# A transformer block on one core: all input transposed by the host, norm factors of the first batches spread on TensorE, weights centred during the load

## The chip, the core and the metric

The kernel runs on one NeuronCore of a Trainium2 chip. Its engines have queues of their own and work in order: TensorE (PE in the profile; its weight loads are the row PEld), VectorE (DVE), ScalarE (ACT), GpSimd (POOL) and SyncE (SP), which issues most DMAs. Matmul results land in PSUM, everything else lies in SBUF or in HBM. The metric is the device time of one execution in microseconds (us); the median of three runs of the kernel before is 656.8.

## The reference

Sixteen batches of 256 tokens with 256 features, all float32. One transformer block with norms ahead of its two halves: attention with 16 heads of width 16, in which a token sees all tokens up to 16 places behind it, and a gated feed-forward net of width 1024, whose weights are interpolated from control points by a cubic.

```python
def layernorm(x):                       # no gain, no bias
    return (x - mean(x)) / sqrt(var(x) + 1e-5)

x = L0_attn_x                           # [16, 256, 256]
n = layernorm(x)
q, k, v = n @ wq.T, n @ wk.T, n @ wv.T  # 16 heads of 16
scores = (q . k) * 16 ** -0.5
scores = where(j - i > 16, -inf, scores)
x = x + (softmax(scores) @ v) @ wo.T
n = layernorm(x)
gate_w, up_w, down_w = spline(gate_cp), spline(up_cp), spline(down_cp)
out = x + (silu(n @ gate_w.T) * (n @ up_w.T)) @ down_w.T
```

## The kernel before

**Stages.** The loop over steps `s` (from 0 to 19) works on several batches at once: in step `s` the row maxima of batch `s-1`, the exponentials and value products of batch `s-2`, the output projection of batch `s-3`, the feed-forward net of batches `s-3` and `s-4`, and the projections of a batch some steps ahead. A step has seven gaps, numbered 1 to 7, between the pieces of the scores; `project(s, gap)` and `fill(s, gap)` put other work there. For the first seven batches (`RAW = 7`) a hand-written table, `early`, says in which step and gap each stage runs; later batches follow the short list in `project`.

**Order.** Every instruction goes out through the wrapper `InOrder`, so each engine keeps the order of the program, and all of these instructions carry line 88 in the profile. They are told apart by tile names.

**Queues and buffers.** PSUM has two score tiles, which stay (`scores`, four banks in all), a ring `ps_f` of two buffers (tag `f`) and a ring `ps_m` of two buffers (tag `m`). A tile of a ring can be written only when the tile two before it has been read. The spline part (`part(i)`, `spline`) takes two of `ps_f` and two of `ps_m` at once, and copies the results with ScalarE (`act.copy`) and then with VectorE (`copy_predicated`). DMAs are issued on SP; the three weights of the projections and half of batch 0's spread are issued on ScalarE's queue. Each DMA takes the next of eight semaphores in turn, and waits for the DMA that had it last.

**The norm ahead of attention** is done in two ways. For batches 0 to 6, VectorE takes mean and variance (`stats_a`), GpSimd the power -1/2 (`rstd`), VectorE makes the normalised `xna` (`norm_a`), TensorE transposes it in four pieces and ScalarE (for batch 1 VectorE) copies the result to `xT` (`turn_a`). From batch 7 on, `xT` comes transposed from the host (`load_xT`), is multiplied with the weights as it is, and the norm's factor is applied to the results: `send_factors` and `spread_factors` write it to HBM and read it back over all partitions, and `project_part` and `project_v` multiply by it. The mean needs no step of its own there, since the columns of the weights have been centred: `sum_weights` (products with a matrix of 1/256) and `center` (a subtraction on VectorE) do this to Wq and Wk in step 3 and to Wv in step 4, when no normalised batch needs them any more.

**Spread.** `spread(b)` sends q and k of a batch with eight DMAs from the copy `qkc` to the layout of the scores, `qk`. The maxima (`find_max`, one VectorE instruction `z` and a short read `mx` behind it for each head) read the score tiles; the next scores wait until they and the exponentials are done.

**At the start**, ahead of the loop, TensorE runs 14 products of the identity (`run`), while the first loads land.

## Time and profile before

| | |
|---|---|
| runs, median of three (lowest to highest) | 656.8 us (655.59 to 658.14) |
| the profiled execution | 656.36 us |
| its span, first to last instruction | 654.3 us |
| TensorE busy | 644.9 us, 99% of the span |
| VectorE, ScalarE, GpSimd busy | 369.0, 216.3, 129.5 us (56%, 33%, 20%) |
| granted TensorE clock, mean | 1.000 |
| moved by DMA | 33.18 MB, mean 51 GB/s |

The profile shows one execution. Its time-ordered list has one row for each run of like instructions on an engine: the start from the begin of the span, the time from the first one's start to the last one's end, the engine, the operation, the tile written and the tiles read, their shapes, the count, and in brackets how long the engine had been idle before and what it then waited for. A float32 matmul shows as two records, one for each of its passes, and a float32 transpose as one. The ends of matmuls are modelled and overlap the next ones, so what a group of them costs TensorE is the distance from its start to the start of the next group.

The engines by stretches of the span (us of busy time):

| stretch, us | TensorE | VectorE | ScalarE |
|---|---|---|---|
| 0 to 17.20 (first scores) | 14.65 | 10.44 | 3.90 |
| 17.20 to 42.14 (step 1) | 24.53 | 20.33 | 8.29 |
| 42.14 to 68.28 (step 2) | 24.59 | 15.88 | 15.59 |
| 68.28 to 93.26 (step 3) | 23.45 | 16.66 | 12.59 |
| 93.26 to 120 | 26.74 | 16.47 | 8.60 |

### The profile page before, as it was taken

What the parts mean: (1) busy time and instruction counts of PE and PEld (TensorE: products, weight loads), DVE (VectorE), ACT (ScalarE), POOL (GpSimd) and SP (SyncE); (2) the same over time, 40 slices, a digit from 0 to 9 for tenths busy, and PEclk for the clock granted to TensorE, in tenths of its full rate; (3) what the DMA queues carried; (4) which work ended last, traced back from release to release, by engine and by line L of the source; (5) the groups of instructions that cost most, each with busy time, mean ns of one, the idle gap of its engine ahead of it and who ended that gap; (6) DMA issues with size and microseconds to landing.
All of it is one profiled execution on the core that took longest, in us unless ns stands there. A gap on an engine that the chain in (4) does not pass through costs nothing.

```text
span 654.3 us, 18421 instructions
## 1 busy us (share of the span) xinstructions
PE 644.9 (99%) x7380; PEld 501.3 (77%) x7380; DVE 369.0 (56%) x1482; ACT 216.3 (33%) x383; POOL 129.5 (20%) x254
## 2 busy tenths in 40 slices
PE   8999999999999999999999999999999999999998
PEld 6666667877878777787877778787777777777886
DVE  6785566656464665646566464655656564733342
ACT  1345533233332323333232333323333333333110
POOL 6232222211111221112121121211212030212000
PEclk9999999999999999999999999999999999999999
DMA  5844132214132231413213131210010101010100
GB/s 170 174 69 63 46 64 65 46 37 87 31 75 42 45 65 36 86 33 73 44 36 75 36 71 33 56 31 18 21 34 20 33 23 31 23 36 19 50 17 16
DMA packets 40612, 33.18 MB, mean 51 GB/s; under 512 B 10576, under 2 KB 39888, under 8 KB 40528
## 3 DMA queue, kind: packets, MB, share of 16 engines
q1 hardware_dynamic: 39392, 30.97, 21.3%
q8 instruction: 58, 0.95, 0.6%
q10 hardware_dynamic: 1136, 1.05, 0.6%
q14 instruction: 26, 0.21, 0.3%
HBM read 14.42 MB, written 4.47 MB: 29 GB/s over the span
## 4 chain that ended last, share of the span: by engine, by line
PE 89%; DVE 1%; ACT 1%; issue 0%; POOL 0%; ACTq 0%
PE pg L88 18%; PE pd L88 17%; PE pu L88 17%; PE scores L88 14%; PE po L88 7%; PE py L88 5%; PE pv L88 3%; PE pq L88 3%; PE pk L88 3%; PE ptf L88 1%; PE pw L88 1%; PE pm L88 0%; ACT e L88 0%; DVE z L88 0%; DVE x L88 0%
## 5 line engine op out<-in xcount | busy, mean ns | idle before, releaser
L88 ACT ACTIVATE e<-scores 128x512 f32<-128x512 f32 (+1 forms) x192 | 117.5, 615 | 273.1 <-PE scores L88 224.5
L88 DVE CUSTOM_DVE_ANT_0 z<-scores,mask 128x144 bf16<-128x144 f32 (+1 forms) x512 | 154.7, 362 | 55.5 <-PE scores L88 32.7
L88 POOL TENSOR_SCALAR_AFFINE_SELECT e<-e 128x224 f32<-128x224 f32 (+1 forms) x192 | 93.8, 489 | 407.2 <-ACT e L88 404.4
L88 PE MATMUL pg<-x2T,gateT 128*128 128x256 f32 x512 | 125.5, 388 | 0.1
L88 PE MATMUL pu<-x2T,upT 128*128 128x256 f32 x512 | 121.0, 379 | 0.0
L88 PE MATMUL pd<-downT,inter 128*128 128x256 f32 x512 | 119.4, 383 | 0.0
L88 DVE SCALAR_TENSOR_TENSOR th<-th,pg 128x512 f32<-128x512 f32 x64 | 44.0, 687 | 117.5 <-ACT th L88 117.5
L88 PE MATMUL scores<-qk 17*64 17x144 f32 (+7 forms) x4096 | 106.2, 317 | 1.6 <-ACT e L88 1.1
L88 PEld LDWEIGHTS pg<-x2T,gateT 128*128 128x128 f32 x512 | 92.5, 190 | 19.7 <-DVE mx L88 4.7
L88 PEld LDWEIGHTS pu<-x2T,upT 128*128 128x128 f32 x512 | 97.3, 190 | 13.2
L88 PEld LDWEIGHTS pd<-downT,inter 128*128 128x128 f32 x512 | 95.2, 190 | 14.5 <-DVE mx L88 0.9
L88 PEld LDWEIGHTS scores<-qk 17*64 17x64 f32 (+1 forms) x4096 | 68.8, 131 | 37.3 <-issue 31.1
L88 ACT ACTIVATE th<-pg 128x512 f32<-128x512 f32 x64 | 38.2, 597 | 69.8 <-PE pg L88 69.2
L88 DVE TENSOR_TENSOR inter<-th,pu 128x512 f32<-128x512 f32 x64 | 44.0, 688 | 26.2 <-PE pu L88 26.2
L88 PE MATMUL po<-e,v 128*32 128x256 f32 (+1 forms) x1024 | 50.0, 336 | 0.0
L88 PEld LDWEIGHTS po<-e,v 128*32 128x32 f32 x1024 | 29.5, 109 | 23.3 <-issue 12.3
L88 DVE DVE_READ_ACCUMULATOR2_ANT mx<- 128x1 f32 x512 | 42.6, 83 | 0.1
L88 DVE TENSOR_TENSOR x<-x,pd 128x256 f32<-128x256 f32 x32 | 13.4, 420 | 41.2 <-PE pd L88 39.9
L88 PE MATMUL pq<-xT,wq 128*128 128x256 f32 x128 | 31.7, 390 | 0.7 <-ACT xT L88 0.7
L88 PE MATMUL py<-wo,ac 128*128 128x256 f32 x128 | 31.9, 392 | 0.0
L88 PE MATMUL pv<-wv,xT 128*128 128x256 f32 x128 | 30.7, 384 | 0.4 <-ACT qkc L88 0.4
L88 PE MATMUL pk<-xT,wk 128*128 128x256 f32 x128 | 30.6, 381 | 0.0
(69 smaller groups left out, 382.9 us busy)
## 6 DMA issues: line engine op xcount, KB each, us to landing
qk<-qkc SPq DMA_DIRECT2D x124, 64.0 KB
x<-x SPq DMA_DIRECT2D x16, 256.0 KB
ac<-au SPq DMA_DIRECT2D x128, 32.0 KB
rb<-rd SPq DMA_DIRECT2D x32, 128.0 KB
out<-x SPq DMA_DIRECT2D x15, 256.0 KB
xT<-xT SPq DMA_DIRECT2D x9, 256.0 KB
fa<-ra SPq DMA_DIRECT2D x9, 128.0 KB
qk<-mxT SPq DMA_DIRECT2D x64, 4.0 KB
```

The lines of the kernel that those rows point to most:

```text
L88: return self.tc.keep_in_program_order(fn(*args, **kwargs))
```

## The change

- All sixteen batches of `xT` are now loaded from the host's transposed input, those of the first seven too, in a pool of five buffers instead of three (`sb5`). The loads of batches 0 to 4 stand beside those of `x`, batches 5 and 6 are loaded in step 1, gap 2, and step 2, gap 2.
- Wq, Wk and Wv are centred ahead of the loop and by step 0: `sum_weights` multiplies with ones instead of 1/256, and `center` scales by -1/256 and adds in one instruction.
- For batches 0 to 6, `norm_a` no longer makes `xna`. ScalarE multiplies the identity by the norm's factor (`diag`), and two products of `ones` with this diagonal (`pfa`) give the factor along the free axis in every partition. For batches 1 to 6, `turn_a` multiplies `xT` with it in place, on VectorE. For batch 0, ScalarE copies it to SBUF (`fa`), and VectorE multiplies q and k with it as they leave PSUM; v of batch 0 is scaled by ScalarE.
- `keep_running` runs 8 products instead of 14. `xnf` has one buffer instead of two. The choice between ScalarE and VectorE for the copies (`copied`) is gone: v of batch 0 leaves PSUM on ScalarE.

```diff
     def load_xT(b):
-        xTs[b] = sb3.tile([P, 2, S], F32, tag="xT", name=f"xT{b}")
+        xTs[b] = sb5.tile([P, 2, S], F32, tag="xT", name=f"xT{b}")
...
-    load_x(0)
...
+    load_x(0)
+    load_xT(0)
     load_x(1)
+    load_xT(1)
...
     load_x(2)
+    load_xT(2)
 
     def load_rest(_):
         load_x(3)
+        load_xT(3)
         sp.dma_start(cp_in[:, 1, :], cps[1])
         load_x(4)
+        load_xT(4)
...
-    means = const.tile([P, P], F32, tag="means", name="means")
-    pool.memset(means, 1.0 / DIM)
+    ones = const.tile([P, P], F32, tag="ones", name="ones")
+    pool.memset(ones, 1.0)
...
     def norm_a(b):
-        xns[b] = normed(b, "a")
-
-    def turn_a(b, engine=act):
-        xTs[b] = sb3.tile([P, 2, S], F32, tag="xT", name=f"xT{b}")
-        transposed(xns.pop(b), xTs[b], f"ta{b}", engine)
+        _, factor = moments[b, "a"]
+        diagonals[b] = sb.tile([P, 2, P], F32, tag="diag", name=f"diag{b}")
+        for c in range(2):
+            act.activation(diagonals[b][:, c, :], ident, AF.Copy, scale=factor[:, c : c + 1])
+
+    def spread_here(b, pool_, tag):
+        _, factors[b] = moments.pop((b, "a"))
+        to = pool_.tile([P, S], F32, tag=tag, name=f"pfa{b}")
+        diagonal = diagonals.pop(b)
+        for c in range(2):
+            pe.matmul(
+                to[:, c * P : (c + 1) * P], lhsT=ones, rhs=diagonal[:, c, :], start=True, stop=True
+            )
+        return to
+
+    def times(dst, src, factor):
+        dve.tensor_tensor(dst, src, factor.unsqueeze(1).to_broadcast([P, 2, S]), ALU.mult)
+
+    def turn_a(b):
+        times(xTs[b], xTs[b], spread_here(b, ps_m, "m"))
...
-                sums[nm], lhsT=means, rhs=w_in[nm][:, kc, :], start=(kc == 0), stop=(kc == 1)
+                sums[nm], lhsT=ones, rhs=w_in[nm][:, kc, :], start=(kc == 0), stop=(kc == 1)
...
-            dve.tensor_tensor(
-                w_in[nm][:, kc, :], w_in[nm][:, kc, :], sums[nm], ALU.subtract
-            )
+            dve.scalar_tensor_tensor(
+                w_in[nm][:, kc, :], sums[nm], -1.0 / DIM, w_in[nm][:, kc, :], ALU.mult, ALU.add
+            )
...
+    def take_products(b, i):
+        qkc, pq = qkcs[b], pqs.pop((b, i))
+        if 0 < b < RAW:
             act.copy(qkc[:, i], pq)
         else:
-            dve.tensor_tensor(
-                qkc[:, i], pq, across[b].unsqueeze(1).to_broadcast([P, 2, S]), ALU.mult
-            )
+            times(qkc[:, i], pq, across[b])
...
     early = {
-        (0, 1): ((stats_a, 1), (value_ones, 1)),
+        (0, 1): ((value_ones, 1),),
         (0, 2): (
-            (norm_a, 1), (project_qk, 0), (spread, 0), (load_rest, 0), (coefficients, 0),
-            (stats_a, 2), (scores_and_values, 2),
+            (load_rest, 0), (coefficients, 0), (stats_a, 2), (scores_and_values, 2),
         ),
-        (0, 4): ((turn_a, 1, dve), (project_v, 0, dve), (norm_a, 2), (part, 0)),
+        (0, 4): ((turn_a, 1), (project_v, 0), (norm_a, 2), (part, 0)),
...
-        (1, 2): ((project_part, 1, 1), (spread, 1), (coefficients, 1)),
+        (1, 2): ((project_part, 1, 1), (spread, 1), (coefficients, 1), (load_xT, 5)),
...
-        (2, 2): ((project_part, 4, 0), (stats_a, 6)),
+        (2, 2): ((project_part, 4, 0), (load_xT, 6), (stats_a, 6)),
...
-        (3, 6): ((project_v, 6), (sum_weights, "q"), (sum_weights, "k")),
-        (3, 7): ((center, "q"), (center, "k")),
-        (4, 1): ((sum_weights, "v"), (center, "v")),
+        (3, 6): ((project_v, 6),),
     }
...
-    keep_running(14)
+    keep_running(8)
     scores_and_values(0)
     constants()
     minus_ones(1)
     stats_a(0)
     norm_a(0)
-    turn_a(0)
+    for nm in "qk":
+        sum_weights(nm)
+        center(nm)
+    project_products(0, 0)
+    across[0] = sb3.tile([P, S], F32, tag="fa", name="fa0")
+    act.copy(across[0], spread_here(0, ps_f, "f"))
+    project_products(0, 1)
+    sum_weights("v")
+    stats_a(1)
+    for i in range(2):
+        take_products(0, i)
+    norm_a(1)
+    spread(0)
+    center("v")
     for s in range(B + 4):
```

More of the change, by code (lines that the diff above doesn't have):

```diff
@@ L117, in block_kernel @@
     sb4 = ctx.enter_context(tc.tile_pool(name="sb4", bufs=4))
+    sb5 = ctx.enter_context(tc.tile_pool(name="sb5", bufs=5))
     sb6 = ctx.enter_context(tc.tile_pool(name="sb6", bufs=6))
@@ L232, in normed @@
         mv, rstd = moments.pop((b, nm))
-        xn = sb.tile([P, 2, DIM], F32, tag=f"xn{nm}", name=f"xn{nm}{b}")
+        xn = sb1.tile([P, 2, DIM], F32, tag=f"xn{nm}", name=f"xn{nm}{b}")
         for c in range(2):
@@ L239, in normed, with transposed @@
         return xn
-    def copied(engine, dst, src):
-        (act.copy if engine is act else dve.tensor_copy)(dst, src)
-    def transposed(src, dst, nm, engine=act):
+    def transposed(src, dst, nm):
         pt = ps_m.tile([P, 2, S], F32, tag="m", name=f"p{nm}")
@@ L253, in transposed @@
                 )
-        copied(engine, dst, pt)
+        act.copy(dst, pt)
     def stats_a(b):
@@ L263, in block_kernel @@
     RAW = 7
+    diagonals = {}
     def norm_a(b):
-        xns[b] = normed(b, "a")
-    def turn_a(b, engine=act):
-        xTs[b] = sb3.tile([P, 2, S], F32, tag="xT", name=f"xT{b}")
-        transposed(xns.pop(b), xTs[b], f"ta{b}", engine)
+        _, factor = moments[b, "a"]
[15 more added lines that the diff above has]
+        times(xTs[b], xTs[b], spread_here(b, ps_m, "m"))
     sums = {}
@@ L297, in spread_factors, with project_products @@
         across[b] = to
-    def project_part(b, i):
+    pqs = {}
+    def project_products(b, i):
         if i == 0:
             qkcs[b] = sb.tile([P, 2, 2, S], F32, tag="qkc", name=f"qkc{b}")
-        nm, qkc = "qk"[i], qkcs[b]
-        pq = ps_m.tile([P, 2, S], F32, tag="m", name=f"p{nm}{b}")
+        nm = "qk"[i]
+        pqs[b, i] = pq = ps_m.tile([P, 2, S], F32, tag="m", name=f"p{nm}{b}")
         for oc in range(2):
@@ L313, in project_part @@
                 )
-        if b < RAW:
+    def take_products(b, i):
+        qkc, pq = qkcs[b], pqs.pop((b, i))
+        if 0 < b < RAW:
             act.copy(qkc[:, i], pq)
         else:
-            dve.tensor_tensor(
-                qkc[:, i], pq, across[b].unsqueeze(1).to_broadcast([P, 2, S]), ALU.mult
-            )
+            times(qkc[:, i], pq, across[b])
+    def project_part(b, i):
+        project_products(b, i)
+        take_products(b, i)
     def project_qk(b):
@@ L333, in spread, with project_v @@
                 )
-    def project_v(b, engine=act):
+    def project_v(b):
         pv = ps_m.tile([P, 2, DIM], F32, tag="m", name=f"pv{b}")
@@ L348, in project_v @@
             heads = pv[:, c, :].rearrange("p (h d) -> p h d", d=HD)
-            if b < RAW:
-                copied(engine, to, heads)
+            if 0 < b < RAW:
+                act.copy(to, heads)
             else:
```

## The prediction

> **What bounds the kernel now.** I read three views in turn: the page's chain of work that ended last, the time-ordered list of TensorE in the first 110 us, and the same list for all engines at the places the change touches. The chain:

> ```profile
> PE 89%; DVE 1%; ACT 1%; issue 0%; POOL 0%; ACTq 0%
> ```

> The end is set by TensorE's queue: what counts is the work in that queue and the holes in it. Slices of 36 us from 120 to 228 us show TensorE busy 35.98 to 36.00 us; nothing that changes there is touched. The question is the first 104 us. After 17.2 us its holes are few (0.70 us at 44.2, 0.38 at 55.2, 0.36 at 63.4, 0.38 at 83.2, 1.04 at 91.7), so removed matmuls pay only where they don't lie in front of such a hole, and a new wait pays in full unless a later hole swallows it.

> **The change part by part, by the order of instructions of both kernels.**

> *Transposes against products of ones.* Per batch 1 to 6, four transposes of 128 columns leave and two full float32 products of 128 columns come. Two rows price them:

> ```profile
> 6.27 0.83 PE L88 MATMUL run<-ident 128*128 128x128 f32 x6
> 30.85 0.65 PE L88 MATMUL pta<-ident,xna 128*128 128x128 f32 x4
> ```

> The `run` products have the shape of the new ones: each is two passes (28 records for 14 products); six passes take 0.83 us, with the last alone 0.274, so one starts every (0.83-0.274)/5 = 0.11 us. Four passes: 0.44. The transposes: (0.65-0.273)/3 = 0.126 apart, four 0.50. [...] The row says -0.06 each, -0.4 in all. [...]

> *Sums of the weights leave steps 3 and 4.* Twelve passes of 256 columns, at 0.22 us: 2.6 us of queue. But where do they lie?

> ```profile
> 89.40 1.03 PE L88 MATMUL sumq<-wq,means 128*128 128x256 f32 x4
> 90.26 1.03 PE L88 MATMUL sumk<-wk,means 128*128 128x256 f32 x4
> 91.12 0.60 PE L88 MATMUL ptf<-ident,xnf 128*128 128x128 f32 x4
> 91.52 0.65 ACT L88 ACTIVATE e<-scores 128x576 f32<-128x576 f32 x1 [3.18 <-DVE mx L88]
> 92.07 0.64 ACT L88 COPY v<-pv 128x256 f32<-128x256 f32 x2
> 92.59 0.62 ACT L88 COPY x2T<-ptf 128x512 f32<-128x512 f32 x1
> ```

> The next gate product waits for x2T (93.26). ScalarE's queue makes x2T: an exponential that waits for VectorE's maxima until 91.52, two v copies, then x2T. None needs sumq or sumk; ptf could start once xnf is there (about 90.5), 0.6 us sooner, and x2T would still come third. So these eight passes fill a hole: gain 0 (1.7 at most). sumv is different: it starts at 99.43, straight behind the values products, and gate products follow at 100.40. Gain 0.9. The six VectorE subtractions (0.37 us apart) lie beside waiting (VectorE idles 2.22 us at 93.7): 0.

> *The start.* Before: `run` to 7.1, transposes, q and k of batch 0 to 12.6, their spread issued at 13.28, transposes of batch 1, v, spline part 0, first scores at 17.21, of which twelve passes wait for the spread until 17.89. After, with durations of these rows: eight `run` products are 16 passes; before 6 us they are 0.213 apart (22 passes between 1.43 and about 6.1), so they end at 4.85. Wq: SP's load of x2 waits for its landing and is issued at 4.98, so sumq starts at 5.0; its first two passes at 0.43, then 0.22: end 6.45. sumk (Wk lands near 6.0 by the bytes of ScalarE's queue) ends 7.3; centring q on VectorE 6.6 to 7.4; pq 7.3 to 9.15; the factor's products to 9.6, its copy (0.37) to 10.2; pk to 11.45; sumv to 12.35. VectorE multiplies q (0.69) after the copy and k when pk is done, 11.65 to 12.35: the spread is issued 0.9 us sooner than 13.28. Then VectorE in order: centring v 13.25, coefficients 0.68, statistics of batch 2 1.35, xT of batch 1 times its factor 0.69, end 16.05. The third spline product needs that buffer and the fourth the one v leaves (ScalarE, 16.05; before: VectorE, 16.05), so scores start at 17.2 as before, now without the DMA wait (0.6). But ScalarE now makes v and the diagonal of batch 2 ahead of the spline copies, so VectorE's predicated copies end at 18.7 instead of 18.3, and step 1's maxima, statistics, maxima with the new 0.69 multiplication between them end at 23.7 instead of 22.96. TensorE waits there: scores at 23.8, not 23.36. Start as a whole: **+0.45**.

> [...]

> *Step 1, gap 5: a new wait.* Spline part 1 takes two of the small ring's two buffers; the last product must wait for the buffer that batch 3's transposes hold:

> ```profile
> 31.11 0.42 DVE L88 CUSTOM_DVE_ANT_0 z<-scores,mask 128x256 bf16<-128x256 f32 x1
> ...
> 31.54 0.59 ACT L88 COPY xT<-pta 128x512 f32<-128x512 f32 x1 [0.50 <-PE pta L88]
> ...
> 32.18 0.29 PEld L88 LDWEIGHTS pw<-cp_in,tab_in 32*128 32x128 f32 x2 [0.44 <-ACT xT L88]
> ...
> 33.23 0.75 PE L88 MATMUL scores<-qk 16*64 16x80 f32 x32
> ```

> An idle ScalarE released it at 32.13. After, the release is VectorE's multiplication, queued behind the four maxima of the same stage (31.11 to 32.5): 32.5 + 0.69 = 33.2. The last spline product, and all of TensorE behind it, starts 1.05 us later: **+1.05**. On VectorE behind it stand the predicated copies, coefficients and the outer maxima; the removed normalisation (0.72 at 34.45) pays for those, so pm at 37.73 no longer waits its 0.15: -0.15. If VectorE came free sooner, the cost would be 0.

> *What else moves.* xna (2 x 0.37) leaves VectorE for the 0.69 multiplication: even. At step 2, gap 1, two multiplications stand behind maxima that end at 44.80 and finish at 46.2; the next maxima began at 46.31. At step 3 one ends at 71.7, the next maxima begin at 72.64. Both covered; uncovered, 0.7 and 1.4. Diagonals on ScalarE: by the 128x256 copies (0.33) at most 0.3 each, against the 0.59 copy that leaves. Loads: seven of 256 KB more, about 0.46 us of SP each. The DMA engines carry 380 GB/s from 4 to 9.3 us, so three more end near 11.4; x2 is needed at 14.0, xT of batch 1 at 15.3. xT3 and xT4 stretch the second burst (16 to 23.7) by 1.4 us; behind it is the spread of batch 1, first read at 42.1. xT5 stands ahead of batch 2's spread on SP, which then ends at 36.0; maxima follow at 38.5. xT6 is issued near 47 and needed after 70. All 0. One buffer for xnf instead of two: its reader is done one step earlier, 0.

> Sum: +0.45 + 1.05 - 0.15 - 0.9 = **+0.45**, taken as +0.4 with the start's rounding. The profiled execution took 656.36 (span 654.3); the runs' median 656.8 stands 0.4 above it. On the median: **657.2 us**.

> **Rivals.**
> - *The queue gets shorter.* All twelve passes pay (-2.6), and the wait at 33 us is absorbed because VectorE arrives sooner: +0.45 - 2.6 - 0.4 = -2.55, 654.2. For: holes move with VectorE's load, which falls at 40 us. Against: the order of instructions puts the maxima ahead of the multiplication, and x2T depends on ScalarE. Chance 0.23.
> - [...] Chance 0.15.
> - [...] Chance 0.09.

> **How the numbers follow.** Forecast 0.53. A measurement of this kernel can tell about 0.5%, 3.3 us, from no change. Faster by more needs the first rival and a start without loss: 0.11. Slower by more: the clock rival mostly, with part of the third and the forecast's tail: 0.18. Within: 0.71. Range 653.8 (first rival less its rounding) to 660.6.

> **What would show it.** First scores near 17.2, and step 1's outer scores near 23.8, released by VectorE; the second loading of spline part 1 near 33.6 behind an `xT` multiplication of VectorE, scores 1.5 us later than 33.23; the first gate product at a distance from py as before (93.26-84.56 = 8.7) with a hole where sumq and sumk stood; the next gate products 0.9 closer behind the values. Wrong would be: the 8.7 falling by 1.7, `run` pitch 0.213 still seen after 7 us, or products of ones 0.22 apart.

## The result, and the profile after

| | before | changed |
|---|---|---|
| median of 11 runs each, us | 657.53 | 660.51 |
| lowest to highest | 655.59 to 658.64 | 657.79 to 662.29 |
| the profiled execution; its span | 656.36; 654.3 | 660.67; 658.9 |
| granted TensorE clock, mean of the profiled execution | 1.000 | 0.992 |

The ratio is 1.0048, with a 95% interval of 1.0031 to 1.0064: the change costs about 3.0 us. The time lies inside the range forecast, but it is a loss that can be measured, where a rise of 0.4 us, too small to be told from nothing, was forecast. In the page of the changed kernel these are the span, the busy times, the clock in 40 slices, and the head of the chain of waits:

```profile
span 658.9 us, 18424 instructions
PE 648.1 (98%) x7368; PEld 502.5 (76%) x7368; DVE 365.4 (55%) x1473; ACT 217.3 (33%) x392; POOL 129.8 (20%) x254
PEclk9999799999999999999999999999999999999999
PE 89%; DVE 1%; ACT 1%; issue 0%; POOL 0%; ACTq 0%
```

TensorE still sets the end, by the same 89% of the chain. New is the 7 in the clock row, in the slice from 66 to 82 us: TensorE's clock was not fully granted there. The stretches show a second place. Columns: stretch, its length, busy time of each engine with its instructions, then granted clock, DMA share and GB/s:

```profile
core 0: us, PE busy (x) PEld busy (x) DVE busy (x) ACT busy (x) POOL busy (x), PEclk, DMA share, GB/s
60.00:72.00 12.00, 11.53 (x106) 5.25 (x96) 6.03 (x22) 5.70 (x12) 1.27 (x2) 0.82 0.31 48
72.00:84.00 12.00, 12.00 (x162) 9.00 (x163) 7.15 (x39) 5.99 (x11) 3.45 (x7) 0.89 0.12 27
84.00:90.00 6.00, 5.62 (x107) 3.73 (x106) 3.20 (x16) 3.15 (x7) 1.51 (x3) 1.00 0.64 139
90.00:96.00 6.00, 4.33 (x79) 3.02 (x77) 4.81 (x23) 1.50 (x3) 1.66 (x3) 1.00 0.40 68
96.00:108.00 12.00, 11.14 (x96) 8.33 (x97) 4.66 (x20) 4.42 (x10) 2.08 (x4) 0.86 0.12 24
```

A halved clock over part of a stretch gives these means. The trace's own clock records give 0.5 at 67.72 to 74.55 us and at 98.44 to 101.85 us: two windows of 3.41 us on end, and one. The profiled execution of the kernel before shows 1.00 in all five stretches; three of them, in the same columns:

```profile
60.00:72.00 12.00, 11.53 (x134) 5.74 (x132) 8.22 (x34) 7.54 (x15) 2.04 (x4) 1.00 0.30 48
90.00:96.00 6.00, 4.85 (x25) 3.81 (x25) 3.78 (x23) 2.62 (x6) 0.69 (x2) 1.00 0.20 18
96.00:108.00 12.00, 12.00 (x135) 9.14 (x134) 8.56 (x29) 3.48 (x6) 2.21 (x5) 1.00 0.11 27
```

What the windows cost is read from the time-ordered list of TensorE in the changed kernel (start, time, engine, operation, count, idle before):

```profile
16.84 0.69 PE L88 MATMUL scores<-qk 16*64 16x208 f32 x16
22.96 0.75 PE L88 MATMUL scores<-qk 16*64 16x80 f32 x32
30.45 0.71 PE L88 MATMUL pfa<-diag,ones 128*128 128x128 f32 x4
31.09 1.13 PE L88 MATMUL pw<-cp_in,tab_in 32*128 32x512 f32 x6
32.90 1.12 PE L88 MATMUL pw<-cp_in,tab_in 32*128 32x512 f32 x2 [0.68 <-DVE xT L88]
33.95 0.75 PE L88 MATMUL scores<-qk 16*64 16x80 f32 x32
64.98 5.23 PE L88 MATMUL pw<-cp_in,tab_in 32*128 32x512 f32 x16
70.14 1.85 PE L88 MATMUL scores<-qk 16*64 16x208 f32 x32
88.55 1.99 PE L88 MATMUL py<-wo,ac 128*128 128x256 f32 x8
94.34 0.78 PE L88 MATMUL ptf<-ident,xnf 128*128 128x128 f32 x4 [0.79 <-DVE xnf L88]
96.76 0.39 PE L88 MATMUL pm<-ident,mx 128*16 128x128 f32 x2 [1.64 <-ACT v L88]
97.25 2.65 PE L88 MATMUL pg<-x2T,gateT 128*128 128x256 f32 x8
99.69 2.96 PE L88 MATMUL pu<-x2T,upT 128*128 128x256 f32 x8
102.59 1.04 PE L88 MATMUL scores<-qk 16*64 16x208 f32 x32
105.05 1.99 PE L88 MATMUL pg<-x2T,gateT 128*128 128x256 f32 x8
```

The same places in the kernel before:

```profile
31.43 1.86 PE L88 MATMUL pw<-cp_in,tab_in 32*128 32x512 f32 x8
64.07 4.28 PE L88 MATMUL pw<-cp_in,tab_in 32*128 32x512 f32 x16
68.28 1.04 PE L88 MATMUL scores<-qk 16*64 16x208 f32 x32
84.56 1.99 PE L88 MATMUL py<-wo,ac 128*128 128x256 f32 x8
92.77 0.39 PE L88 MATMUL pm<-ident,mx 128*16 128x128 f32 x2 [1.04 <-ACT v L88]
93.26 1.99 PE L88 MATMUL pg<-x2T,gateT 128*128 128x256 f32 x8
95.09 1.89 PE L88 MATMUL pu<-x2T,upT 128*128 128x256 f32 x8
100.40 1.89 PE L88 MATMUL pg<-x2T,gateT 128*128 128x256 f32 x8
```

Side by side:

| start of | before, us | changed, us | later by |
|---|---|---|---|
| first scores | 17.21 | 16.84 | -0.37 |
| outer scores of step 1 | 23.36 | 22.96 | -0.40 |
| scores behind spline part 1 | 33.23 | 33.95 | +0.72 |
| spline parts 4 and 5 (`pw` x16) | 64.07 | 64.98 | +0.91 |
| output projection (`py`) of step 3 | 84.56 | 88.55 | +3.99 |
| first gate products | 93.26 | 97.25 | +3.99 |
| next scores | 96.91 | 102.59 | +5.68 |
| next gate products | 100.40 | 105.05 | +4.65 |
| end of the span | 654.3 | 658.9 | +4.6 |

The jumps of 3.08 and 1.69 us lie where the clock is halved: 32 passes of scores take 1.85 us at 70.14 and 1.04 at 102.59. Together they are 4.77 us, a little more than the 4.6 at the end, so in this execution the rest of the change comes to about -0.1.

**Counting half-clock windows.** One execution says little about how often this happens, but each timed run has its mean clock. A window of these records is 3.413 us at 0.5, which takes 0.0026 from the mean over 656 us, and the means do cluster in such steps: 1.000, 0.997, 0.995, 0.992, 0.989. So every run tells its number of windows. The mean span of the kernel before, over the 156 runs beside the experiments, was 654.7 us with none (70 runs), 656.3 with one (49), 657.4 with two (30), 659.1 with three (4) and 659.7 with four (3): 1.4 us a window by a straight line through all runs. It had 0.92 windows a run (standard error 0.08). The changed kernel had 2.60 (0.31), and none of its runs was without.

### The profile page after: what moved, and what is told of

It reads as the page before. It is cut to its first block, busy times and chain, and to the rows that moved or that the text cites. A ratio compares the mean times of both kernels' runs of the same rounds, so it can differ in the third digit from the quotient of the medians.

```text
span 658.9 us, 18424 instructions
## 1 busy us (share of the span) xinstructions
PE 648.1 (98%) x7368; PEld 502.5 (76%) x7368; DVE 365.4 (55%) x1473; ACT 217.3 (33%) x392; POOL 129.8 (20%) x254
## 3 DMA queue, kind: packets, MB, share of 16 engines
q10 hardware_dynamic: 1136, 1.05, 0.6%
## 4 chain that ended last, share of the span: by engine, by line
PE 89%; DVE 1%; ACT 1%; issue 0%; POOL 0%; ACTq 0%
PE pg L88 18%; PE pd L88 17%; PE pu L88 17%; PE scores L88 14%; PE po L88 7%; PE py L88 5%; PE pv L88 3%; PE pq L88 3%; PE pk L88 3%; PE ptf L88 1%; PE pw L88 1%; PE pm L88 0%; ACT e L88 0%; DVE z L88 0%; DVE x L88 0%
## 5 line engine op out<-in xcount | busy, mean ns | idle before, releaser
L88 ACT ACTIVATE e<-scores 128x512 f32<-128x512 f32 (+1 forms) x192 | 117.4, 615 | 275.6 <-PE scores L88 226.8
L88 DVE CUSTOM_DVE_ANT_0 z<-scores,mask 128x144 bf16<-128x144 f32 (+1 forms) x512 | 154.6, 362 | 53.7 <-PE scores L88 34.6
L88 POOL TENSOR_SCALAR_AFFINE_SELECT e<-e 128x224 f32<-128x224 f32 (+1 forms) x192 | 94.3, 492 | 410.7 <-ACT e L88 409.6
L88 PE MATMUL pg<-x2T,gateT 128*128 128x256 f32 x512 | 126.2, 389 | 0.1
L88 PE MATMUL pu<-x2T,upT 128*128 128x256 f32 x512 | 122.0, 381 | 0.0
L88 PE MATMUL pd<-downT,inter 128*128 128x256 f32 x512 | 119.4, 383 | 0.0
L88 DVE SCALAR_TENSOR_TENSOR th<-th,pg 128x512 f32<-128x512 f32 x64 | 44.0, 688 | 121.5 <-ACT th L88 121.5
L88 PEld LDWEIGHTS pu<-x2T,upT 128*128 128x128 f32 x512 | 98.2, 192 | 13.7
L88 PEld LDWEIGHTS pg<-x2T,gateT 128*128 128x128 f32 x512 | 92.7, 190 | 19.9 <-DVE mx L88 4.7
L88 PE MATMUL scores<-qk 17*64 17x144 f32 (+7 forms) x4096 | 106.3, 319 | 1.5 <-ACT e L88 1.0
L88 PEld LDWEIGHTS pd<-downT,inter 128*128 128x128 f32 x512 | 95.2, 190 | 14.5 <-DVE mx L88 0.9
L88 PEld LDWEIGHTS scores<-qk 17*64 17x64 f32 (+1 forms) x4096 | 69.0, 131 | 37.5 <-issue 32.5
L88 ACT ACTIVATE th<-pg 128x512 f32<-128x512 f32 x64 | 38.2, 597 | 69.9 <-PE pg L88 69.3
L88 DVE TENSOR_TENSOR inter<-th,pu 128x512 f32<-128x512 f32 x64 | 44.0, 688 | 27.3 <-PE pu L88 27.3
L88 PE MATMUL po<-e,v 128*32 128x256 f32 (+1 forms) x1024 | 51.2, 342 | 0.0
L88 PEld LDWEIGHTS po<-e,v 128*32 128x32 f32 x1024 | 30.0, 111 | 24.3 <-issue 13.6
L88 DVE DVE_READ_ACCUMULATOR2_ANT mx<- 128x1 f32 x512 | 42.5, 83 | 0.1
L88 DVE TENSOR_TENSOR x<-x,pd 128x256 f32<-128x256 f32 x32 | 13.4, 420 | 41.9 <-PE pd L88 41.9
L88 PE MATMUL py<-wo,ac 128*128 128x256 f32 x128 | 31.9, 392 | 0.0
L88 PE MATMUL pq<-xT,wq 128*128 128x256 f32 x128 | 31.7, 390 | 0.2 <-DVE gateT L88 0.2
L88 PE MATMUL pv<-wv,xT 128*128 128x256 f32 x128 | 30.7, 384 | 0.5 <-ACT qkc L88 0.5
L88 PE MATMUL pk<-xT,wk 128*128 128x256 f32 x128 | 30.6, 381 | 0.0
```

The source lines that it names most:

```text
L88: return self.tc.keep_in_program_order(fn(*args, **kwargs))
```

## The experiments

Two theories were to be told apart. **The clock**: stretches where TensorE has little to do bring half-clock windows behind them, and the change opens two such stretches, the hole in step 3 where `sumq` and `sumk` stood, and the new wait at 32 us. **The queue**: the loss is the wait itself and work moved, and the windows come as they like.

### The sums back in step 3

Eight passes of `sumq` and `sumk`, whose results nobody reads, return to the place they had; nothing else.

```diff
-        (3, 6): ((project_v, 6),),
+        (3, 6): ((project_v, 6), (sum_weights, "q"), (sum_weights, "k")),
```

> The changed kernel, with the eight passes of sumq and sumk put back in step 3, gap 6, as products that nobody reads. Theory (the clock): in the changed kernel TensorE does too little between 93 and 98 us, and the granted clock halves for one window of 3.4 us behind it; with the eight passes the hole is filled, the clock stays at 1.0 between 97 and 102 us, and the time falls by 1 to 1.7 us against the changed kernel's 660.5, to about 659, although TensorE has 1.7 us more to do. Rival (queue length): the passes lie in a hole and change nothing in the time; the clock row shows the dip as before. Second rival: they are on the path, +1.7.

Measured: median 659.40 us in 22 runs, ratio 1.0023 (1.0010 to 1.0036); 1.63 windows a run (0.15) instead of 2.60. TensorE around the hole in this kernel, in an execution without any window (the only one of the 22):

```profile
90.50 1.03 PE L88 MATMUL sumq<-wq,ones 128*128 128x256 f32 x4
...
92.22 0.60 PE L88 MATMUL ptf<-ident,xnf 128*128 128x128 f32 x4
93.87 0.39 PE L88 MATMUL pm<-ident,mx 128*16 128x128 f32 x2 [1.05 <-ACT v L88]
94.36 1.99 PE L88 MATMUL pg<-x2T,gateT 128*128 128x256 f32 x8
96.19 1.89 PE L88 MATMUL pu<-x2T,upT 128*128 128x256 f32 x8
```

More work in TensorE's queue makes the kernel faster, by 1.1 us. The up products take 1.89 us here, at full clock, against 2.96 in the halved window behind the open hole. That such windows come less often with the hole filled is told by the counts, not by this one execution.

### The sums taken from the kernel before

```diff
-        (3, 6): ((project_v, 6), (sum_weights, "q"), (sum_weights, "k")),
-        (3, 7): ((center, "q"), (center, "k")),
+        (3, 6): ((project_v, 6),),
```

> The kernel before, with sumq, sumk and the centring of Wq and Wk in step 3 left out, so q and k of batches 7 to 15 are made from weights that are not centred. Theory (the clock): the hole in step 3 opens as in the changed kernel, the clock halves behind it, and the kernel becomes 1 to 1.7 us slower than before. Rival (queue length): TensorE has 1.7 us less to do, so 0 to 1.7 us faster.

Measured: 657.63 us, ratio 1.0011 (0.9993 to 1.0030), 22 runs; 1.09 windows (0.26), against 0.92. At no window the span is 654.4 against 654.7: as queue time the sums were worth next to nothing. But the windows hardly rose, so the experiment did not show what the clock theory wanted. The runs spread wider (655.92 to 663.85), and the one profiled had three windows: at 68.5 us behind the spline parts, at 95.8 us behind the opened hole, and at 403.0 us. The last stands behind a hole of 1.96 us at 399 us, which the profiled execution of the kernel before does not have and whose cause the trace does not show. The hole in step 3 was tried again below.

### Batch 3's multiplication a gap earlier

To take the wait at 32 us away, `turn_a(3)` runs one gap sooner.

```diff
-        (1, 4): ((project_v, 1), (stats_a, 4)),
-        (1, 5): ((turn_a, 3), (part, 1), (norm_a, 4), (coefficients, 2)),
+        (1, 4): ((project_v, 1), (turn_a, 3), (stats_a, 4)),
+        (1, 5): ((part, 1), (norm_a, 4), (coefficients, 2)),
```

> The changed kernel with the factor multiplication of batch 3 one gap earlier (step 1, gap 4), ahead of the maxima that it stood behind. Theory (wait): the hole of 0.68 us at 32.2 us goes, the last product of spline part 1 starts about 32.2, and the span is 0.6 to 0.8 us shorter at an equal clock. Rival: the maxima come later by as much and TensorE waits for them instead; no change. The clock's dips near 68 and 98 us are not touched by it, so the whole time falls by at most 1 us.

A miss: 660.95 us, ratio 1.0061 (1.0032 to 1.0091), 3.04 windows (0.42) in 7 runs. TensorE there:

```profile
30.78 1.35 PE L88 MATMUL pw<-cp_in,tab_in 32*128 32x512 f32 x8
33.75 0.75 PE L88 MATMUL scores<-qk 16*64 16x80 f32 x32 [1.61 <-DVE mx L88]
```

The spline products run through, but the multiplication now stands ahead of the maxima on VectorE, and the scores wait for these: the hole grew from 0.68 to 1.61 us, and a third dip of the clock, to 0.50, appeared right behind it, at 35.0 to 38.4 us.

### Fillers among the spline products

The first dip, from 67.72 us, lies behind spline parts 3 to 5, which both kernels have. TensorE looks busy there (11.53 of the 12 us from 60 to 72), but the profile gives the spline products as `32*128`, a quarter of the `128*128` of the products of the identity. Fillers are products of the identity with itself, written to a score tile that the next scores overwrite: 8 passes behind part 3, 8 behind part 4. The sums stand in step 3 as above.

```diff
+    def keep_busy(n):
+        for _ in range(n):
+            pe.matmul(tiles[0][:, 0, 0:P], lhsT=ident, rhs=ident, start=True, stop=True)
...
-        (2, 6): ((project_v, 3), (part, 3)),
-        (2, 7): ((part, 4), (part, 5)),
+        (2, 6): ((project_v, 3), (part, 3), (keep_busy, 4)),
+        (2, 7): ((part, 4), (keep_busy, 4), (part, 5)),
```

> The changed kernel with the eight passes of sumq and sumk in step 3 and, in addition, eight passes of products of the identity after each of spline parts 3 and 4 (62 to 67 us), where TensorE waits for copies. Theory (the clock): both dips go, the mean clock is 0.997 to 1.0, and the time is about 655 to 656 (span 653.5 to 654.5), below both kernels, with about 3.5 us more matmul work in the queue. Rival (the dips come from something else, the length of the start or chance): the clock stays near 0.992 and the time rises by up to 2 us from the added passes.

Measured: 658.28 us, ratio 1.0014 (0.9998 to 1.0030); 0.84 windows (0.18) against 1.63 with the sums alone. The fillers behind part 3 are on the path and cost some 0.57 us; 1.1 us is gained all the same. The time of 655 to 656 us that was expected is missed: a third place was left, the wait at 32 us.

### The wait at 32 us taken away

ScalarE, idle there, copies batch 3's factor out of PSUM, so that the buffer comes free without VectorE, which multiplies from the copy later. Once in the changed kernel, once with the sums in step 3 besides.

```diff
-        times(xTs[b], xTs[b], spread_here(b, ps_m, "m"))
+        factor = spread_here(b, ps_m, "m")
+        if b == 3:
+            kept = sb3.tile([P, S], F32, tag="fa", name=f"fa{b}")
+            act.copy(kept, factor)
+            factor = kept
+        times(xTs[b], xTs[b], factor)
```

> The changed kernel; for batch 3 alone, the factor leaves PSUM by a copy on ScalarE, and VectorE multiplies from that copy, so the buffer that the last product of spline part 1 needs is free as early as before. Theory (the wait): the hole of 0.68 us at 32.2 us goes and TensorE's queue is 0.6 to 1 us shorter from there on. Theory (the clock): a sparse stretch of TensorE goes too, so the mean number of half-clock windows in a run (each 3.413 us, 0.0026 of the mean clock) falls from the changed kernel's 2.5 by 0.3 to 0.7; the time falls by 1 to 2 us in all, to about 659. Rival (queue length alone): mean clock as in the changed kernel, time down by 0.6 to 1.

> The run before with, in addition, the eight unread passes of sumq and sumk in step 3. Theory (the clock): with both sparse stretches that the change made gone, the mean number of half-clock windows is that of the kernel before (about 1), and the median equals the kernel before's, or is up to 0.7 below it. Rival (another part of the change lowers the clock or lengthens the queue): it stays at 1.5 windows or more, and 1 us or more above the kernel before.

TensorE at that place in the first of the two:

```profile
30.64 0.71 PE L88 MATMUL pfa<-diag,ones 128*128 128x128 f32 x4
31.28 1.65 PE L88 MATMUL pw<-cp_in,tab_in 32*128 32x512 f32 x8
32.86 0.75 PE L88 MATMUL scores<-qk 16*64 16x80 f32 x32
```

From the spline products to the scores it is 1.58 us, against 2.86 in the changed kernel (31.09 to 33.95): 0.68 of hole, and the rest because six products and then two take 1.13 + 1.12 us where eight together take 1.65. The first kernel's median is 657.64 us, ratio 0.9996 (0.9979 to 1.0012), with 1.72 windows (0.27); with the sums besides it is 656.55, ratio 0.9985 (0.9971 to 0.9998), with 0.98 (0.17). So the wait costs twice: its own time, and 0.65 (with the sums) to 1.04 of a window (without, both sets of runs of the changed kernel taken together). Without the sums that is more than the 0.3 to 0.7 of a window expected, and the time fell by 2.9 us, not by 1 to 2. At no window the spans are 653.4 and 653.2 us, 1.3 to 1.5 below the kernel before.

### All three places filled, and the fillers alone in the kernel before

The wait taken away, the sums in step 3, 4 passes of filler behind part 3 and 8 behind part 4, and 8 passes behind step 3's transposes (20 passes of filler, not the 22 of the expectation):

```diff
+        (2, 6): ((project_v, 3), (part, 3), (keep_busy, 2)),
+        (2, 7): ((part, 4), (keep_busy, 4), (part, 5)),
...
+        if s == 3:
+            keep_running(4)
```

> The run before with fillers in addition: products of the identity behind spline part 3 (four passes), behind part 4 (eight) and behind the transposes of step 3 (eight). Theory (the clock): half-clock windows fall to 0.3 a run or fewer, and the median is 655.5 to 656.5 us, 1 us or more below the kernel before, with 22 passes more in the queue. [...]

The second kernel is the one before, with the two `keep_busy` alone.

> The kernel before with the same fillers behind spline parts 3 and 4 alone. Theory (the clock): most of its own half-clock windows come from the stretch of spline parts 3 to 5, so they fall from about 1 a run to 0.3, and the median falls by 0.8 to 1.3 us. Rival: windows are as before and the time rises by 0.1 to 0.5 us.

Measured: 655.66 us, ratio **0.9963 (0.9951 to 0.9975)**, 0.09 windows a run (0.06); 21 of 22 runs have none. This version is faster than both kernels. The fillers alone bring the kernel before from 0.92 to 0.11 windows (0.08), 657.06 us, ratio 0.9985 (0.9970 to 1.0000). TensorE in step 3 of the full version:

```profile
91.22 0.60 PE L88 MATMUL ptf<-ident,xnf 128*128 128x128 f32 x4
91.66 1.06 PE L88 MATMUL run<-ident 128*128 128x128 f32 x8
92.86 0.39 PE L88 MATMUL pm<-ident,mx 128*16 128x128 f32 x2 [0.15 <-ACT v L88]
93.35 1.99 PE L88 MATMUL pg<-x2T,gateT 128*128 128x256 f32 x8
```

Eight useless passes fill the 1.05 us hole; the gate products wait for ScalarE as before and start 8.69 us behind the output projection (84.66), so the path is not lengthened.

### Step 3 opened again, with the other places filled

In both kernels of the last pair the sums (and what stands with them: the centring in the first, the fillers behind the transposes in the second) leave step 3 again, so that it is the only sparse stretch left.

> The kernel before with the fillers behind spline parts 3 and 4 and without sumq, sumk and the centring of Wq and Wk (so q and k of batches 7 to 15 are made from weights that are not centred): of the sparse stretches only the hole in step 3 is left. Theory (a sparse stretch of step 3 halves the clock by itself): 0.6 to 0.9 half-clock windows a run, against 0.1 with the sums; the time rises by 0.8 to 1.4 us. Rival (the hole in step 3 costs windows only in the changed kernel): 0.1 to 0.3 windows, time as with the sums.

> The changed kernel with the early release at 32 us and the fillers behind spline parts 3 and 4, and nothing added in step 3: only the hole in step 3 is left. Theory: 0.6 to 0.9 half-clock windows a run, against 0.1 with the step filled; median 1 us or so above the 655.7 of the kernel with all fillers. Rival: 0.1 to 0.3 windows, median at 655.7 or below.

From the kernel before: 0.11 windows become 1.04 (0.13), 657.86 us, ratio 1.0002 (0.9992 to 1.0012). From the full version: 0.09 become 0.84 (0.22), 656.17 us, ratio 0.9972 (0.9959 to 0.9986). The stretches of the second:

```profile
85.00:92.00 7.00, 5.25 (x83) 3.82 (x81) 5.81 (x31) 2.09 (x5) 2.05 (x4) 1.00 0.40 67
92.00:99.00 7.00, 6.31 (x16) 4.76 (x17) 0.95 (x5) 2.08 (x6) 0.64 (x1) 0.51 0.20 39
99.00:106.00 7.00, 7.00 (x93) 4.99 (x99) 4.15 (x16) 2.29 (x4) 1.46 (x3) 1.00 0.04 8
```

From 92 to 99 us the clock is halved, and 16 matmul records fill 6.31 us. So the hole in step 3 brings 0.75 to 0.93 windows where nothing else disturbs it. At no window the spans hardly differ without and with the sums (654.7 and 654.9; 653.4 and 654.0, the latter with the fillers' own time): the effect of these eight passes is the clock. In the second pair the time rose by 0.5 us only, half of what was expected, since the fillers that went had a cost of their own.

### The changed kernel again

> The changed kernel itself, for more executions on the chip that runs the others. Theory: 2.2 to 2.8 half-clock windows a run and a span that, extrapolated to none, is 0 to 0.8 us above the kernel before's. Rival (the first eleven executions were unlucky): 1.5 windows or fewer and a median below 659.5.

660.92 us in 11 runs, ratio 1.0044 (1.0026 to 1.0063), 2.92 windows (0.27), a little above the 2.2 to 2.8 expected: the loss and its windows come again.

### The three places together

| kernel | spline parts | step 3 | wait at 32 us | windows a run | median, us |
|---|---|---|---|---|---|
| changed (22 runs, both sets) | open | open | there | 2.76 | 660.5 and 660.9 |
| sums in step 3 | open | filled | there | 1.63 | 659.40 |
| wait taken away | open | open | none | 1.72 | 657.64 |
| both | open | filled | none | 0.98 | 656.55 |
| fillers, sums | filled | filled | there | 0.84 | 658.28 |
| all three, step 3 open | filled | open | none | 0.84 | 656.17 |
| all three | filled | filled | none | 0.09 | 655.66 |
| before | open | filled | none | 0.92 | 657.8 (156 runs) |
| before, fillers | filled | filled | none | 0.11 | 657.06 |
| before, fillers, step 3 open | filled | open | none | 1.04 | 657.86 |
| before, step 3 open | open | open | none | 1.09 | 657.63 |

Pairs of rows that differ in one place differ by 0.65 to 1.13 windows; only the last row stands out, 0.17 from the kernel before and 0.05 from the row above it.

**What stood ahead of the halved windows.** The profiles of the changed kernel and of the kernel before say more than the busy time does. In the changed kernel the clock records begin at 6.28 us (at 1.0), 67.72 (0.5), 74.55 (1.0), 98.44 (0.5) and 101.85 us (1.0): 18, 2, 7 and 1 times 3.413 us apart. For every stretch of 3.413 us on that grid the work that TensorE did can be worked out: the columns of all passes, at the measured 0.22 us for 256 of them (0.43 where the clock is halved), weighted by the rows and columns that each record names as active, as a share of 128 x 128 (32 rows in a spline product, 16 or 17 rows and 64 columns in a score product). By this estimate the stretch before 67.72 us holds 0.35 of what passes of 128 x 128 without a break would hold, the halved one behind it, which a second halved one follows, 0.24, and the one before 98.44 us 0.33. All others of this profile, apart from the end of the span, hold 0.38 or more. In the kernel before's, where the first clock record runs from 6.25 to 654.78 us at 1.0, the lowest on the grid of its own records, again apart from the end, holds 0.45. TensorE's busy time does not part them (stretch, its length, TensorE's busy time with its passes, granted clock, DMA share and GB/s, in the changed kernel):

```profile
30.17:33.59 3.42, 2.75 (x28) 1.00 0.57 134
64.31:67.72 3.41, 2.94 (x14) 1.00 0.60 91
67.72:71.13 3.41, 3.41 (x31) 0.50 0.04 9
95.03:98.44 3.41, 1.67 (x9) 1.00 0.23 21
```

Behind the first of these stretches, which holds 0.38, the clock stays at 1.00; the other three have a halved window behind them, one after 1.67 us of work and one after 3.41. This reading was made after the experiments, from two profiles, and no run was made to test it; it gives no limit that holds beyond them.

## Why the prediction was wrong

**The failed step** is the price of the cover that left step 3. The prediction says of `sumq` and `sumk`: "these eight passes fill a hole: gain 0 (1.7 at most)". The queue side of it held: the first gate product stands 8.70 us behind the output projection, to the hundredth as forecast. But filling the hole was what these passes were worth. The same step left out the clock a second time at the new wait, which was priced at its own 1.05 us. The clock was weighed at the start alone, as a rival, though the views showed a kernel with few holes that runs at a clock of 1.000, and the change made two more holes. By the counts above the changed kernel has 2.76 - 0.92 = 1.84 windows more; at 1.4 us each that is some 2.6 us, of a loss of 3.0. The base of the forecast was off as well: the kernel before takes 657.53 us over 11 runs, not the 656.8 of three, which makes 0.7 of the 3.3 us between the forecast and the measured time.

The idle times themselves gave no warning: the longest in front of the window at 98.44 us are 0.79 and 1.64 us, both shorter than the 3.413 us that the clock was halved for.

**Step by step, what was forecast and what came:**

- *The start*: +0.45 forecast, -0.4 measured (16.84 and 22.96 in the table). `sumq` ran from 5.00 to 6.50 us, as forecast (5.0 to 6.45). What was too long were the steps on VectorE: its statistics begin at 4.16 us instead of 4.65, as x of batch 0 lands earlier, and batch 0's spread is issued at 12.2, not 0.9 but 1.1 us sooner; the predicated copies end at 18.3, not 18.7, so the new multiplication does not delay the outer scores.
- *The wait in step 1*: +1.05 forecast. From the start of the spline products to the scores it was 1.80 us before (31.43 to 33.23) and is 2.86: +1.06, released by the multiplication that was named, 0.7 us sooner than the time given for it (32.90 against 33.6), because the start is early. The 0.15 said to come back does not show: of the gain, nothing is seen by 65 us, where the delay is 0.91.
- *`sumv`*: -0.9 forecast; the next gate products come 1.03 us closer (+5.68 to +4.65).
- *Products of ones for transposes*: the sum counts nothing for them, and the row held. From `pfa` at 30.45 to the spline products 0.64 us, from `pta` at 30.85 before 0.58: +0.06 a batch.
- *The sum of the queue*: +0.45 forecast. The profile leaves -0.1 beside the clock; the mean spans at one, two and three windows over both sets of runs (656.4, 658.7 and 659.4 us, against 656.3, 657.4 and 659.1) leave +0.1 to +1.3, and two profiles at full clock, the sums in step 3 against the kernel before (655.2 and 654.3), +0.9. The sum has the right sign and size, in part by luck: the start was priced too dear, and the wait seems to cost more than at its place, since taking it away shortens the span at equal windows by 1.3 to 2.0 us.
- *The rivals*: the shorter queue fell with the 8.70 us. The chances of 0.15 and 0.09 stand for a clock halved through the start and for products of ones dearer than the transposes, and no run shows either: the first scores came early, at 16.84 us instead of 17.21, and the products of ones cost 0.06 us a batch. The halved clock had been thought of there, at the wrong place.

**Still open.** Why the kernel before, with step 3 opened and the spline parts unfilled, has hardly more windows (1.09) than with it closed (0.92), while with fillers the same cut brings 0.93 more. A dip at the spline parts shifts step 3 by some 1.5 us (half of the 3.08 us that two windows cost above) against the grid, which could matter; this was only argued, not tried, and in the profiled run both dips came. Nor is it settled whether the share of 128 x 128 is what the clock follows, or something that goes with it. What the repaired wait pays beyond the 1.28 us at its place, up to 0.7, may come from a wait for a DMA of the maxima at 98 us that some traces have (0.38 us with the sums in step 3, 0.44 us with all three places filled); it was not isolated.

## What to carry to other kernels

Before useless or early work is taken from a TensorE queue, look at what the stretch holds without it: a hole that costs nothing in the queue can cost 1.4 us a time by the clock (the line through the 156 runs of the kernel before), and a few products without use can be the cheapest fix. Read the mean clock of every timed run beside its time; here it sorted runs that seemed noise into steps, and compared kernels at an equal number of half-clock windows. A wait of TensorE, in a kernel that it bounds, is priced twice: by its length and by the clock behind it (here 1.28 us at its place, and 0.65 to 1.04 windows a run).
